# Product for the row maxima moved into the third chunk, scans paced by step, chunks and projection moved into the first and last steps of an attention loop

## The chip, the cores and the metric

The kernel runs on one core of one Trainium2 chip, in fp32. The metric is the device time of one execution in microseconds (us); lower is better. The core's engines are called PE (TensorE, matrix products), DVE (VectorE), ACT (ScalarE), POOL (GpSimd) and SP (SyncE, which here only issues DMA transfers). Each works through its own queue of instructions in order and waits on semaphores for the others.

## The reference, cut to what matters

The inputs are `x` [4, 256, 256] (4 batches, 256 tokens, width 256) and a context [4, 4096, 256]. In short:

```
x = x + cross_attention(x, ctx)     # 8 heads of 64, keys and values from 256 own rows and 4096 context rows
x = x + mixed(x)                    # per batch: a router picks 64 tokens for self-attention (16 heads);
                                    # the other 192 go through a state space model (512 channels, 16 states)
x = x + mixture_of_experts(x)       # 8 experts, 2 per token, hidden width 512
```

with layer norms ahead of the parts. In the state space model a recurrence h_t = dA_t * h_(t-1) + dBu_t runs along the 192 tokens for each channel and state. Cross-attention is by far the largest part, and the change lies in the loop that computes it.

## The kernel before: a loop over 128 steps

**Steps and groups.** The attention loop (L1546 to L1650) runs `n` from 0 to `N + 1`, `N` = 128. A group `G = n // 8` is one batch and one pair of heads (16 groups); a step `s = n % 8` is 32 query rows of it, for two heads. The 4352 keys lie as four quarters of 1088 on the partitions, so a score tile is 128 x 1088 for each head.

In step `n` the queues get, in this order:

- `scores(n)` (L1377): 32 + 4 products on PE into PSUM, tile `su`.
- `exps(n - 1)` (L1425): exponentials of the step before on ACT, with the negated maxima `nb` as bias.
- `copy_max(n)` (L1397): two passes of DVE over 128 x 1088 that copy `su` to `sp` and take the row maxima, then a small product into `mq` (L1410).
- pieces of other work on PE: key chunks of the next group (`k_chunk`, L1323) in s = 0, 6 and 7, value chunks of this group (`v_chunk`, L1354) in s = 2, 3 and 4, and in s = 1 and 5 `values` (L1442), the product of the exponentials with the values for four steps, cut into four pieces.
- `stat(n)` (L1412): the product of `mq` with `same`, which brings the four quarters' maxima together in a corner of `su`, and a reduction on DVE to `nb` (L1420). Since scores and this product share `su`, the scores of step n + 1 wait for `nb`.
- `turn(n - 1, 0)` and `turn(n - 1, 1)` (L1436): DVE transposes of the exponentials, which `values` reads.

Every chunk of keys or values reads 512 context rows, loaded over SP's queue into one of four buffers (`load_ctx`, L1235).

**Row sums and normalization.** When a group is through, `sums` and `spread` write the reciprocal row sums to DRAM, `fetch` (L1486, issued from ACT's queue in s = 1 of the next group) reads them back broadcast as `rs`, and `normalize` (L1502) multiplies the outputs `ao` by them on DVE. When a batch is through, `finish_batch` projects its four head pairs and adds to `x_sb`.

**Background work.** The mixed layer of batch b runs beside the attention of batch b + 1 (batch 3's in the expert stage behind the loop). It is written as Python generators: `slot(budget)` (L1169) at a few places of a step lets those go on whose due time (`yield delay, cost`) has come on a hand-kept clock `now` and whose cost on DVE fits the budget. `ssm_scan` (L702) is one of them: 32 scans per batch on DVE (`scan`, L743), each beside two exponentials for `da` on ACT (L731) and four passes on POOL (L736, L749, L751). A scan asks for 1.4 of a slot's budget; a second one in a slot is taken if 1.15 is left. `ssm_back` (L858) projects the result and adds it back; its first products are copied by ACT to `dsort` (L876).

The weights of a group come by `load_qk` (`wk2`), `load_self` (`wself`, one buffer, read by `k_self`, L1336) and `load_v`, all on SP's queue.

**After the loop** the expert stage begins (L1659); its weights reuse the memory of the loop's pools.

Of the kernel before, what the change touches and what calls it, by code (L numbers as in the profile page):

```python
# [14 lines left out]
P = 128  # L15
# [31 lines left out]
def perceiver_layer(ctx: ExitStack, tc: tile.TileContext, a: dict, out: bass.AP):  # L47
# [654 lines left out]
    def ssm_scan(b, st):  # L702

        SG = 2
        xc, delta, y = st["xc"], st["delta"], st["y"]
        das, dbs, bbs, cbs = {}, {}, {}, {}

        def load(k, o):

            if k < K:  # L710
                t = bg.tile(
                    [P, SG, NBOT], F32, tag=("bb", "cb")[o], name=("bb", "cb")[o], bufs=2
                )
                nc.sync.dma_start(
                    out=t, in_=st["bcd"][o, SG * k : SG * (k + 1), :].partition_broadcast(P)
                )
                (bbs, cbs)[o][k] = t

        def make(i):

            k, h = divmod(i, 2)
            if k == K:
                return
            tags = ((("r0", "r1"), ("r2", "r3")), (("wa", "wa"), ("ua", "r4")))[h]
            for j in range(2):
# [12 lines left out]
        def scan(k, m):  # L738

            da, db = das[k, m], dbs[k, m]  # L740
            nc.vector.memset(da[:, 1:, 0:1], 0.0)  # L741
# [12 lines left out]
        load(0, 0)  # L754
        load(0, 1)
        load(1, 0)
        while "attended" not in st:
            yield 1.0, 0
        make(0)
        make(1)  # L760
        yield 5.0, 1.4
        for i in range(2 * K):
            k, h = divmod(i, 2)
            for m in (2 * h, 2 * h + 1):
                if i or m:
                    if room[0] >= 1.15:
                        room[0] -= 1.15
                    else:
                        yield 2.2, 1.4
                scan(k, m)  # L770
                output(k, m)
            if h:
                load(k + 1, 1)
                load(k + 2, 0)
            make(i + 2)
# [82 lines left out]
    def ssm_back(b, st):  # L858
# [11 lines left out]
        for q, n in ((0, P), (1, NBOT - P)):  # L870
            for m in range(NDT):
                nc.tensor.matmul(
                    ps[:n, q * D : (q + 1) * D], zs[:, m, q * P : q * P + n],
                    ow[m // 2][:, m % 2, :], start=(m == 0), stop=(m == NDT - 1),
                )
            nc.scalar.copy(dsort[:n, q, :], ps[:n, q * D : (q + 1) * D])  # L876
        yield 2.5, 0.7

# [8 lines left out]
        nc.vector.tensor_tensor(xb, xb, ps, ALU.add)  # L887

    done = set()
    finished = set()  # L890
    late = {}

    def routed(b):
# [15 lines left out]
        ]  # L909
        if not late:  # L910
            yield 3.0, 0
        yield from st["late"] if late else ssm_scan(b, st)
        while "attended" not in st:
            yield 1.0, 0
        yield from ssm_back(b, st)
# [290 lines left out]
    with ExitStack() as s1:  # L1206
# [113 lines left out]
                ps.rearrange("p (k q i) -> p q k i", q=4, i=32),  # L1320
            )

        def k_chunk(G, g):  # L1323
# [5 lines left out]
            for c in range(KD):  # L1329
                nc.tensor.matmul(  # L1330
                    ps, wqk[G][:, 0, c, :], ct[:, c, :],
                    start=(c == 0), stop=(c == KD - 1),
                )
            keys_out(G, g * (CK // 4), ps)

        def k_self(G):  # L1336
# [14 lines left out]
                    ps[r, :T].rearrange("p (k q i) -> p q k i", q=4, i=32),  # L1351
                )

        def v_chunk(G, g):  # L1354

            b = G // NHP
            n = 4 if g < NCH else 2
            v = wk.tile([P, n, P], F32, tag=f"v{n}", name="v", bufs=NCH if g < NCH else 1)
            ps = ps_m.tile([P, 512], F32, tag="m", name="psv")
            if g < NCH:  # L1360
                ct = load_ctx(b, g)
            for i in range(n):
                for c in range(KD):
                    if g < NCH:
                        lhsT, w = ct[:, c, i * P : (i + 1) * P], 0
# [135 lines left out]
            ao = aos[divmod(G, NHP)][:, q]  # L1501
            nc.vector.tensor_tensor(ao, ao, rss[G][:, q], ALU.mult)  # L1502

        def project(b, half, ps, hps):
            for hp in hps:
                nc.tensor.matmul(
                    ps[:, half * D : (half + 1) * D],
                    aos[b, hp][:, half * P : (half + 1) * P], wo[:, hp, :],
                    start=(hp == 0), stop=(hp == NHP - 1),
                )  # L1510

        def add(b, half, ps):
            xb = x_sb[:, 2 * b + half, :]
            nc.vector.tensor_tensor(xb, xb, ps[:, half * D : (half + 1) * D], ALU.add)

        def finish_batch(b):

            yield 1.0, 0.9
            if b in psx:
                ps, done_hp = psx[b], NHP - 1  # L1520
            else:
                ps, done_hp = bank("psx"), 0
                project(b, 0, ps, range(NHP))
                add(b, 0, ps)
            project(b, 1, ps, range(done_hp, NHP))
            add(b, 1, ps)
            finished.add(b)

        psx = {}

        with tc.manual_schedule():
            norms = {}
# [13 lines left out]
            for n in range(N + 2):  # L1546
# [7 lines left out]
                if s % 4 == 1:  # L1554
                    m, took = n // 4 - 1, 1.95
                    if m >= 0:
                        pieces = [
                            lambda i=i: values(m, i, min(i + 9, NJ)) for i in range(0, NJ, 9)
                        ]
                elif 2 <= s <= 4 and G < NG:  # L1560
                    pieces = [
                        lambda g=g: v_chunk(G, g) for g in range(3 * s - 6, 3 * s - 3)
                    ]
                elif G + 1 < NG:
                    if s == 0:
                        wqk[G + 1] = load_qk(G + 1)
                        wself[G + 1] = load_self(G + 1)
                    pieces = {
                        0: [lambda g=g: k_chunk(G + 1, g) for g in range(3)],
                        6: [lambda g=g: k_chunk(G + 1, g) for g in range(3, 6)],  # L1570
                        7: [lambda: k_self(G + 1)]
                        + [lambda g=g: k_chunk(G + 1, g) for g in range(6, 8)],
                    }[s]


                tail = n >= N - 2

                def piece(i):
                    if i < len(pieces):
                        pieces[i]()  # L1580
                    if i < len(pieces) or tail:
                        now[0] += took

                if new:
                    scores(n)
# [2 lines left out]
                    exps(n - 1)  # L1588
                if new:
                    copy_max(n)  # L1590
                piece(0)
                if s % 4 != 1:
                    slot(1.3)
                    piece(1)
                    if old:
                        turn(n - 1, 0)
                    if new:
                        stat(n)
                        now[0] += 0.3
# [5 lines left out]
                    slot(1.3 if tail else 0.5)  # L1605
                    piece(2)
                    if s == 0 and n:
                        spread(G - 1)
                    slot(2.9)
                else:  # L1610
                    last = s == 1 and G
# [1 line left out]
                    if last:  # L1613
                        fetch(G - 1)
                    piece(1)
                    if new:
                        stat(n)
                        now[0] += 0.3
                    slot(2.8)
                    if last:  # L1620
                        normalize(m - 1)
                    if n == N + 1:

                        psx[B - 1] = bank("psx")
                        project(B - 1, 0, psx[B - 1], range(NHP))
                        add(B - 1, 0, psx[B - 1])
                        project(B - 1, 1, psx[B - 1], range(NHP - 1))
                    piece(2)
                    slot(1.5)
                    piece(3)  # L1630
                    if n > 4:
                        values_out(m)
                    if old:
                        turn(n - 1, 0)
                        turn(n - 1, 1)
# [344 lines left out]
```

## Time and profile before

| | |
|---|---|
| median of 3 runs | 1524.51 us (1523.6 to 1528.17) |
| the profiled execution's own time | 1526.89 us |
| its span | 1525.1 us |
| mean granted clock of PE | 0.981 |
| steps 0 to 127 of the loop | from 24.9 us to about 1242 us |
| expert stage | from about 1272 us on |
| DVE maxima pass, 128 x 1088 (L1403) | 256 of 1282 ns |
| DVE transpose, 128 x 1088 (L1440) | 256 of 1293 ns |
| DVE scan, 128 x 384 (L743) | 96 of 1317 ns |

The 96 scans are those of batches 0 to 2. "PE su L1415 <- DVE mq" reads: PE's product of line 1415, which writes `su`, waited for DVE's instruction that wrote `mq`. In a timeline the bracket holds the engine's idle time ahead of the line and what ended it; "issue" is time in which the engine waited for nothing that the profile shows.

### The profile page before, as it was taken

Reading aid. Unit: us, or ns where it says so; the run is one execution under the profiler, and the core shown is the slowest. Engines: PE = TensorE matmul, PEld = TensorE weight load, DVE = VectorE, ACT = ScalarE, POOL = GpSimd, SP = SyncE. Lnnn points to the kernel's source line nnn. Section 1 sums busy time; section 2 is a strip of 40 time slices with the busy share of each in tenths; the row PEclk is TensorE's granted clock in tenths of the full one; section 3 lists DMA queues with packets and bytes.
Section 4 is the critical chain, followed back from the end, with each engine's and each line's share of the span. In section 5 each row is a group of like instructions: output and inputs, shape, how many; then the busy total and the mean of one; then the engine's idle time right before and its main releaser. Section 6 shows DMA issues by size and latency. Waiting matters only on the chain.

```text
span 1525.1 us, 35283 instructions
## 1 busy us (share of the span) xinstructions
PE 1444.4 (95%) x14630; PEld 1021.4 (67%) x14630; DVE 1061.7 (70%) x1824; ACT 758.6 (50%) x1484; POOL 404.5 (27%) x467
## 2 busy tenths in 40 slices
PE   7999999999999999999999999999998968898999
PEld 3747566677666566676757575767575657888887
DVE  1656665656698986666889956666989663699353
ACT  3444454454665645455766544556655522553311
POOL 1000000000078860000598800001989101111020
PEclk9999999999999999999999999999999979999999
DMA  6555534424445343425454444352543333787661
GB/s 230 156 148 150 162 117 155 156 88 138 136 132 173 122 136 128 157 78 154 145 151 145 147 142 132 105 164 87 191 138 107 105 125 114 218 274 232 222 198 53
DMA packets 160352, 225.42 MB, mean 148 GB/s; under 512 B 15520, under 2 KB 78752, under 8 KB 160192
## 3 DMA queue, kind: packets, MB, share of 16 engines
q1 hardware_dynamic: 149632, 208.96, 43.5%
q10 hardware_dynamic: 9072, 10.13, 2.0%
q0 software_dynamic: 1488, 4.07, 0.9%
q8 instruction: 116, 1.90, 0.5%
q14 instruction: 44, 0.36, 0.1%
HBM read 218.66 MB, written 4.46 MB: 146 GB/s over the span
## 4 chain that ended last, share of the span: by engine, by line
PE 60%; DVE 20%; POOL 9%; issue 5%; DMA 3%; ACT 2%; SPq 0%; ACTq 0%; DVEq 0%; POOLq 0%
PE psv L1368 10%; PE su L1384 10%; PE po L1449 10%; PE psk L1330 9%; DVE sp L1403 6%; DVE db L743 4%; POOL y L751 3%; POOL db L749 3%; POOL db L736 3%; DVE pt L1440 3%; PE su L1391 2%; PE pde L1906 2%; PE pg L1893 2%; PE pu L1893 2%; DVE db L839 2%
## 5 line engine op out<-in xcount | busy, mean ns | idle before, releaser
L1403 DVE TENSOR_SCALAR_CACHE_REDUCE sp<-su 128x1088 f32<-128x1088 f32 x256 | 318.8, 1282 | 186.8 <-PE su L1391 186.8
L1440 DVE STREAM_TRANSPOSE pt<-sp 128x1088 f32<-128x1088 f32 x256 | 327.5, 1293 | 30.6 <-PE po L1449 26.6
L1431 ACT ACTIVATE sp<-sp,nb 128x1088 f32<-128x1088 f32 x256 | 305.1, 1195 | 15.7 <-DVE nb L1420 13.8
L1449 PE MATMUL po<-pt,v 128*64 128x128 f32 x4352 | 261.0, 278 | 2.1 <-DVE pt L1440 1.3
L1384 PE MATMUL su<-kt,qh 64*32 64x512 f32 x4096 | 256.3, 610 | 4.5 <-DVE nb L1420 4.0
L1330 PE MATMUL psk<-ctx,wk 128*128 128x512 f32 x512 | 245.9, 614 | 11.7 <-DMA ctx<-in_ctxT 8.0
L1368 PE MATMUL psv<-wv,ctx 128*128 128x128 f32 x2048 | 252.3, 280 | 0.0
L1449 PEld LDWEIGHTS po<-pt,v 128*64 128x64 f32 x4352 | 242.4, 139 | 11.9 <-issue 6.3
L1368 PEld LDWEIGHTS psv<-wv,ctx 128*128 128x128 f32 x2048 | 237.7, 193 | 11.1 <-issue 8.9
L1330 PEld LDWEIGHTS psk<-ctx,wk 128*128 128x128 f32 x512 | 91.7, 192 | 100.3 <-issue 92.6
L1318 ACT COPY kt<-psk 128x512 f32<-128x512 f32 x128 | 74.6, 585 | 155.8 <-PE psk L1330 155.5
L1384 PEld LDWEIGHTS su<-kt,qh 64*32 64x32 f32 x4096 | 63.1, 108 | 124.0 <-issue 95.5
L1372 ACT COPY v<-psv 128x512 f32<-128x512 f32 x144 | 79.4, 558 | 134.1 <-PE psv L1368 132.8
L751 POOL TENSOR_TENSOR y<-y,db 128x192 f32<-128x192 f32 x192 | 139.7, 728 | 15.0
L743 DVE TENSOR_TENSOR_SCAN db<-da,db 128x384 f32<-128x384 f32 x96 | 126.4, 1317 | 11.4 <-POOL y L751 0.5
L749 POOL TENSOR_TENSOR db<-db,cb 128x384 f32<-128x384 f32 x96 | 108.1, 1126 | 43.6 <-DVE da L741 43.6
L395 POOL TENSOR_TENSOR kbd<-qk,hmask 128x512 f32<-128x512 f32 x8 | 8.6, 1096 | 403.1 <-ACT qk L385 403.1
L731 ACT ACTIVATE da<-delta,A_log_sb 128x192 f32<-128x192 f32 x192 | 75.4, 447 | 51.0 <-DVE da L741 31.5
L736 POOL TENSOR_TENSOR db<-bb,xc 128x384 f32<-128x384 f32 x96 | 99.5, 1059 | 0.2
L1391 PEld LDWEIGHTS su<-kx,qh 128*32 128x32 f32 x1024 | 20.2, 108 | 109.4 <-issue 109.4
L1415 PEld LDWEIGHTS su<-mq,same 128*128 128x128 f32 x256 | 40.8, 190 | 66.3 <-DVE mq L1410 46.9
L1496 ACT COPY ao<-po 128x128 f32<-128x128 f32 x32 | 8.4, 264 | 139.5 <-PE po L1449 139.5
(297 smaller groups left out, 1569.3 us busy)
## 6 DMA issues: line engine op xcount, KB each, us to landing
ctx<-in_ctxT SPq DMA_DIRECT2D x256, 512.0 KB
gateT<-in_gateT SPq DMA_DIRECT2D x27, 512.0 KB
upT<-in_upT SPq DMA_DIRECT2D x27, 512.0 KB
downT<-in_downT SPq DMA_DIRECT2D x27, 512.0 KB
bb<-bcd SPq DMA_DIRECT2D x24, 192.0 KB
cb<-bcd SPq DMA_DIRECT2D x24, 192.0 KB
wv<-in_wv SPq DMA_DIRECT2D x32, 128.0 KB
in_w<-in_in_w SPq DMA_DIRECT2D x32, 128.0 KB
```

The lines of the kernel that those rows point to most:

```text
L736: nc.gpsimd.tensor_tensor(db, bbs[k], bc(xc[:, m, :], 1, SG), ALU.mult)
L743: nc.vector.tensor_tensor_scan(out=db, data0=da, data1=db, initial=0.0, op0=ALU.mult, op1=ALU.add,)
L749: nc.gpsimd.tensor_tensor(db, db, cbs[k], ALU.mult)
L751: nc.gpsimd.tensor_tensor(y[:, m, :], y[:, m, :], db[:, s, :], ALU.add)
L1330: nc.tensor.matmul(ps, wqk[G][:, 0, c, :], ct[:, c, :], start=(c == 0), stop=(c == KD - 1),)
L1368: nc.tensor.matmul(ps[:, i * P : (i + 1) * P], lhsT, wv[G][:, w, c, :], start=(c == 0), stop=(c == KD - 1),)
L1372: nc.scalar.copy(v.rearrange("p k d -> p (k d)"), ps[:, : n * P])
L1384: nc.tensor.matmul(su[q * 32 : (q + 1) * 32, SC[j] + lo : SC[j] + lo + 512], qT[r, s * 32 : (s + 1) * 32], kt[r, q, lo : lo + 512], start= ...
L1403: nc.vector.tensor_scalar(out=sps[n][j], in0=su[:, SU[j] : SU[j] + QK], scalar1=1.0, scalar2=None, op0=ALU.mult, op1=ALU.max, accum_out=nm ...
L1431: nc.scalar.activation(sps[n][j], sps[n][j], AF.Exp, bias=nbs[n][:, j : j + 1], accum_out=lss[b][:, hp, s, j : j + 1],)
L1440: nc.vector.transpose(pts[m, j][:, i, :], sps[n][j])
L1449: nc.tensor.matmul(pos[m][j * HD : (j + 1) * HD, :], vts[m // 2, k // 4][:, k % 4, j * HD : (j + 1) * HD], pts[m, j][:, :, kk * 32 : (kk + ...
```

## The change

1. **The maxima product.** `stat(n)` becomes `maxima()` and is called in the middle of the step's third chunk: after the first of two products of a `k_chunk`, or half way through a `v_chunk`. In s = 1 and 5 it comes after the third piece of `values`, and so in s = 1 after the `normalize` that used to follow it. In the last two steps it comes first.
2. **Pacing.** A slot of 1.3 opens ahead of the first piece, and what is left of it is offered again behind that. While a batch's scans run, the last slot of a step is 1.5 instead of 2.9 in s = 4 and 7 (from n = 97 on only in s = 4), and 1.5 instead of 2.8 in s = 1 and 5. The scan's delay is 1.9 instead of 2.2.
3. **First steps.** In group 0 the first two value chunks move to step 1, and `load_self` of the second group moves from s = 0 to s = 6.
4. **Last steps.** In the last group three value chunks move to its step 0 (n = 120). They lie in a key buffer that is free there (`vfirst`). The projection of the last batch's first three head pairs, and its add, move to n = 126.
5. **`ssm_back`.** The products of both halves come before the two copies to `dsort`.

```diff
-                        yield 2.2, 1.4
+                        yield 1.9, 1.4
...
+        for q, n in ((0, P), (1, NBOT - P)):
             nc.scalar.copy(dsort[:n, q, :], ps[:n, q * D : (q + 1) * D])
...
+        if not late:
+            scanning.add(b)
         yield from st["late"] if late else ssm_scan(b, st)
+        scanning.discard(b)
...
+                if mid and c == 0:
+                    mid()
...
+            if G == NG - 1 and g < 3:
+
+                if g == 0:
+                    vts["first"] = wke.tile([P, 4, SQ], F32, tag="kt", name="vfirst")
+                v = vts["first"][:, g, : n * P].rearrange("p (k d) -> p k d", d=P)
...
+                if mid and 2 * i == n - n % 4:
+                    mid()
...
+            add(b, project(b, range(NHP - 1 if b == B - 1 else 0, NHP)))
...
+                if G == 0 and s == 1:
+                    pieces = [lambda g=g: v_chunk(G, g) for g in range(2)]
+                elif s % 4 == 1:
...
+                elif G < NG and (2 <= s <= 4 or s == 0 and G == NG - 1):
+                    at = {0: (2, 5, 7, 9), NG - 1: (3, 6, 8, 9)}.get(G, (0, 3, 6, 9))
...
+                    if s == (6 if G == 0 else 0):
                         wself[G + 1] = load_self(G + 1)
...
+                if n == N - 2:
+
+                    part = project(B - 1, range(NHP - 1))
+                if tail:
+                    maxima()
+                slot(1.3)
                 piece(0)
                 if s % 4 != 1:
-                    slot(1.3)
+                    slot(room[0])
                     piece(1)
                     if old:
                         turn(n - 1, 0)
-                    if new:
-                        stat(n)
-                        now[0] += 0.3
+                    now[0] += 0.3
+                    slot(1.3 if tail else 0.5)
+                    if tail:
+                        piece(2)
+                    elif len(pieces) > 2:
+                        piece(2, mid=maxima)
+                    else:
+                        maxima()
...
+                    slot(1.5 if scanning and s in ((4,) if n > N - 32 else (4, 7)) else 2.9)
...
                     piece(1)
-                    if new:
-                        stat(n)
-                        now[0] += 0.3
-                    slot(2.8)
+                    now[0] += 0.3
+                    slot(1.5 if scanning else 2.8)
                     if last:
                         normalize(m - 1)
...
                     piece(2)
+                    if not tail:
+                        maxima()
                     slot(1.5)
```

More of the change, by code (lines that the diff above doesn't have):

```diff
@@ L889, in perceiver_layer @@
     done = set()
+    scanning = set()
     finished = set()
@@ L1321, in keys_out, with k_chunk @@
             )
-        def k_chunk(G, g):
+        def k_chunk(G, g, mid=None):
             b = G // NHP
@@ L1352, in k_self, with v_chunk @@
                 )
-        def v_chunk(G, g):
+        def v_chunk(G, g, mid=None):
             b = G // NHP
             n = 4 if g < NCH else 2
-            v = wk.tile([P, n, P], F32, tag=f"v{n}", name="v", bufs=NCH if g < NCH else 1)
+            if G == NG - 1 and g < 3:
[3 more added lines that the diff above has]
+            else:
+                v = wk.tile([P, n, P], F32, tag=f"v{n}", name="v", bufs=NCH if g < NCH else 1)
             ps = ps_m.tile([P, 512], F32, tag="m", name="psv")
@@ L1502, in normalize, with project, add @@
             nc.vector.tensor_tensor(ao, ao, rss[G][:, q], ALU.mult)
[L1504 to L1514, printed above, removed]
+        def project(b, hps):
+            ps = bank("psx")
+            for half in range(2):
+                for hp in hps:
+                    nc.tensor.matmul(
+                        ps[:, half * D : (half + 1) * D],
+                        aos[b, hp][:, half * P : (half + 1) * P], wo[:, hp, :],
+                        start=(hp == hps[0]), stop=(hp == hps[-1]),
+                    )
+            return ps
+        def add(b, ps):
+            for half in range(2):
+                xb = x_sb[:, 2 * b + half, :]
+                nc.vector.tensor_tensor(xb, xb, ps[:, half * D : (half + 1) * D], ALU.add)
         def finish_batch(b):
             yield 1.0, 0.9
[L1519 to L1526, printed above, removed]
+            add(b, project(b, range(NHP - 1 if b == B - 1 else 0, NHP)))
             finished.add(b)
-        psx = {}
         with tc.manual_schedule():
@@ L1553, in perceiver_layer @@
                     wv[G + 1] = load_v(G + 1)
-                if s % 4 == 1:
+                if G == 0 and s == 1:
+                    pieces = [lambda g=g: v_chunk(G, g) for g in range(2)]
+                elif s % 4 == 1:
                     m, took = n // 4 - 1, 1.95
[L1556 to L1560, printed above, removed]
-                    pieces = [
-                        lambda g=g: v_chunk(G, g) for g in range(3 * s - 6, 3 * s - 3)
+                    pieces = [
+                        lambda i=i: values(m, i, min(i + 9, NJ)) for i in range(0, NJ, 9)
+                    ]
+                elif G < NG and (2 <= s <= 4 or s == 0 and G == NG - 1):
+                    at = {0: (2, 5, 7, 9), NG - 1: (3, 6, 8, 9)}.get(G, (0, 3, 6, 9))
+                    if s == 0:
+                        at = (0, at[0])
+                    else:
+                        at = at[s - 2 : s]
+                    pieces = [
+                        lambda mid=None, g=g: v_chunk(G, g, mid) for g in range(*at)
                     ]
@@ L1566, in perceiver_layer, with piece, maxima @@
                         wqk[G + 1] = load_qk(G + 1)
+                    if s == (6 if G == 0 else 0):
                         wself[G + 1] = load_self(G + 1)
                     pieces = {
-                        0: [lambda g=g: k_chunk(G + 1, g) for g in range(3)],
-                        6: [lambda g=g: k_chunk(G + 1, g) for g in range(3, 6)],
+                        0: [lambda mid=None, g=g: k_chunk(G + 1, g, mid) for g in range(3)],
+                        6: [lambda mid=None, g=g: k_chunk(G + 1, g, mid) for g in range(3, 6)],
                         7: [lambda: k_self(G + 1)]
-                        + [lambda g=g: k_chunk(G + 1, g) for g in range(6, 8)],
+                        + [lambda mid=None, g=g: k_chunk(G + 1, g, mid) for g in range(6, 8)],
                     }[s]
                 tail = n >= N - 2
-                def piece(i):
+                def piece(i, **mid):
                     if i < len(pieces):
-                        pieces[i]()
+                        pieces[i](**mid)
                     if i < len(pieces) or tail:
                         now[0] += took
+                def maxima():
+                    if new:
+                        stat(n)
                 if new:
@@ L1596, in perceiver_layer @@
                         turn(n - 1, 0)
-                    if new:
-                        stat(n)
-                        now[0] += 0.3
+                    now[0] += 0.3
[4 more added lines that the diff above has]
+                        piece(2, mid=maxima)
+                    else:
+                        maxima()
                     if s == 0 and n:
@@ L1604, in perceiver_layer @@
                         turn(n - 1, 1)
-                    slot(1.3 if tail else 0.5)
-                    piece(2)
+                    if n == N - 2:
+                        add(B - 1, part)
                     if s == 0 and n:
                         spread(G - 1)
+                    slot(1.5 if scanning and s in ((4,) if n > N - 32 else (4, 7)) else 2.9)
+                elif n == 1:
+                    piece(1)
+                    now[0] += 0.3
+                    turn(0, 0)
+                    maxima()
+                    turn(0, 1)
                     slot(2.9)
@@ L1615, in perceiver_layer @@
                     piece(1)
-                    if new:
-                        stat(n)
-                        now[0] += 0.3
-                    slot(2.8)
+                    now[0] += 0.3
+                    slot(1.5 if scanning else 2.8)
                     if last:
                         normalize(m - 1)
[L1622 to L1627, printed above, removed]
                     piece(2)
+                    if not tail:
+                        maxima()
                     slot(1.5)
                     piece(3)
-                    if n > 4:
-                        values_out(m)
+                    values_out(m)
                     if old:
```

## The prediction

> **What bounds the kernel now.** I read the page first, then the waits of TensorE (PE) and VectorE (DVE), then PE's idle gaps over 0.3 us in order of time, then the timeline around the largest.
>
> ```profile
> PE 1444.4 (95%) x14630; PEld 1021.4 (67%) x14630; DVE 1061.7 (70%) x1824; ACT 758.6 (50%) x1484; POOL 404.5 (27%) x467
> ...
> DVE  1656665656698986666889956666989663699353
> ...
> PEclk9999999999999999999999999999999979999999
> ```
>
> PE is busy 95% of 1525.1 us, so all that reordering can win is its idle 81 us and time at a low clock. DVE's digits reach 9 where the scans of a batch run (slices 12 to 14, 20 to 22, 28 to 30), and there PE's gaps lie. PE's waits, then one of DVE's:
>
> ```profile
> PE su L1415 <- DVE mq L1410: 27.4, 19, 3.4
> PE psk L1330 <- DMA ctx<-in_ctxT: 8.0, 3, 6.3
> ...
> PE su L1415 <- DVE da L741: 4.5, 5, 2.1
> ...
> PE psk L1330 <- issue: 2.4, 1, 2.4
> ...
> PE pssd L872 <- ACT dsort L876: 1.8, 4, 0.5
> ```
> ```profile
> DVE ao L1502 <- DMA rs<-rd: 35.8, 13, 6.5
> ```
>
> The first and the third of PE's lines are one thing: the maxima product (L1415) reaches the head of PE before DVE has made `mq`, with a scan in front of it or behind it. In a quiet step there is no gap: the product comes at 5.8 to 6.3 us of the step, `mq` at 5.08. By batch the gaps are, from the trace: batch 0 0.38, 2.86, 2.10, 0.30, 1.13 (6.8 us); batch 1 2.84, 1.67, 1.14 (5.65); batch 2 2.86, 3.44, 0.72 (7.0): 19.5 us. The smaller ones of each batch's way back (0.9 + 0.9 + 0.6) and the end I take separately.
>
> A gap also costs clock. Stretches just after gaps of 2.38, 2.86 and 2.10 us (PE, PEld, DVE, ACT and POOL busy, then the granted clock):
>
> ```profile
> 30.40:33.70 3.30, 3.30 (x5) 1.35 (x4) 0.00 (x0) 0.59 (x1) 0.00 (x0) 0.50 0.75 286
> 482.40:485.80 3.40, 0.54 (x5) 0.49 (x5) 3.37 (x7) 0.59 (x1) 3.24 (x5) 1.00 0.80 201
> 511.70:515.00 3.30, 3.30 (x32) 3.28 (x33) 3.18 (x4) 2.37 (x6) 2.33 (x3) 0.50 0.29 77
> ```
>
> (the second holds its gap; no drop follows it). A drop lasts 3.4 us at 0.50, so it costs 1.7 us. The Trainium skill ("TensorE: Matmul & The Clock Gate", Part 1: The HAM clock gate) says to allow no idle gaps over about 3.4 us. By it the gaps here but one would be free of clock; the trace shows drops after 2.10 and 2.38 us, and I price a gap over 2 us at 1.7 more. By the rule the scan gaps are worth 19.5 us; by the trace, with five drops (511, 801, 829, 1119, 1170 us), 19.5 + 5 x 1.7 = 28 us.
>
> **The change, part by part.**
>
> *Start.* These lines show the order of SyncE's queue:
>
> ```profile
> 24.42 0.37 SPq L1217 DMA_DIRECT2D wself<-in_wk  x1
> ...
> 24.83 0.47 SPq L1217 DMA_DIRECT2D wself<-in_wq  x1
> ...
> 25.35 9.97 SPq L1235 DMA_DIRECT2D ctx<-in_ctxT  x6
> ...
> 29.55 5.37 PE L1330 MATMUL psk<-ctx,wk 128*128 128x512 f32 x8 [2.38 <-issue]
> ```
>
> The second group's `wself` has one buffer, waits for `k_self(0)`, and holds the ctx loads of step 0 behind it. Moved to step 6, where its two 128 KB loads wait for nothing and are due a step (some 8 us) later, it frees them: 2.38 + 1.7 = -4.1. If the ctx loads are late anyway, 0; the queue is otherwise empty, so I take -4.1.
>
> *Steps 1 to 4.* Step 1 has 3.1 us of gaps now. Two value chunks (8 us of PE) go there, but steps 3 and 4 keep 2 chunks each, and then scores, two maxima (1.28 each), product and `nb` set a floor of 6.5 to 7 us: 28.9 us for the four becomes 28.4, -0.5 (0 to -2.5). The chunks' 512 KB context loads go out a step earlier on SyncE's queue with them, past no other load, and into four buffers that PE frees by then; GpSimd's queue is passed by nothing. The last group's chunks into step 120 fill its 3.44 and 0.72, already counted.
>
> *Product in the third chunk.* It starts 0.4 to 0.8 us later in a step, so `mq` may be that much later. In quiet steps nothing is won. `nb` is later too, and scores(n+1), into the same banks, wait for it: it ends at about 7.2 of 7.8 us, still hidden. Turn(n-1,0) stands ahead of `nb` on DVE in both.
>
> *Pacing of the scans.* 32 scans per batch of 1.317 + 0.12 us each are spread over 16 steps (15 in batch 2) where they took 14. Eight steps then carry 16 x 1.44 = 23 us of scans and 8 x 5.45 us of maxima, `mq`, turns and `nb` = 43.6, in all 67.7 with sums and `ao`; PE needs 67.4 for eight steps. With 18 scans it was some 71. So DVE is level with PE, no longer behind it, and I take 24 of the 28 us away; the bounds are 14 (half the gaps stay, being burst by burst) and 28.
>
> *The new wait.* In steps 8G+1 the built order of DVE's queue is maxima, `mq`, scans, `ao`, `nb`, turns; it was maxima, `mq`, scan, `nb`, scans, `ao`. `ao` (L1502) waits for a DMA and `nb` is now queued behind it; scores(n+1), the whole of PE, wait for `nb`. In step 49 of before:
>
> ```profile
> 474.39 0.52 ACTq L1486 DMA_DIRECT2D rs<-rd  x1
> ...
> 478.79 0.99 DVE L1502 TENSOR_TENSOR ao<-ao,rs 128x128 f32<-128x128 f32 x1 [2.28 <-DMA rs<-rd]
> ```
>
> 4.4 us from issue to use, as in every such step. The issue sits on ACT's queue behind `da` activations, which wait for the first scan after `mq`: in both orders `mq` + 2.1. So `nb` ends at `mq` + 2.1 + 4.4 + 0.3 + 0.15 = `mq` + 7.0. With `mq` at 5.4 to 6.7 of the step that is 12.4 to 13.7, PE's work ends at 10.35: a gap of 2.0 to 3.4 us, with a drop of the clock 3.7 to 5.1. It comes in steps 49, 57, 81, 89, 113, 121, six times. In quiet steps the fetch is issued at 3.9, `ao` is at 8.3 to 8.5 and the product at 8.4 to 8.9 of 10.28 us: hidden. I take 4.2 x 6 = 25 us; bounds 12 and 31. In step 9 the same wait may cost 0.5. Net of pacing and wait: -24 + 25 = +1 (-16 to +17).
>
> *Way back of the scans.* Both products before the copies to `dsort` takes away the 0.46 us wait four times: -1.5, since the copies' next reader stands a step later. The normalization's chains move to other steps, at the same price.
>
> *End.* Three quarters of the last projection go into step 126, which has gaps of 3.03 and 3.03; there its 6 products (1.5 us) hide, and after the last values 2 products and 2 adds remain: -1.4 to the first expert. In step 126 itself -0.5: `pslg` with its normalization comes in its place. The first expert weights' buffers now come free with the last reader of "vfirst", some 21 us after the scores of step 127 begin instead of 4. They are due at 32; three loads of 512 KB at the 195 GB/s of the stage take 8: hidden by 3 us.
>
> Sum: -4.1 - 0.5 + 1 + 0.5 - 1.5 - 0.5 - 1.4 = -6.5 us. Against the profiled execution's 1526.89 (span 1525.1 and 1.8 around it) that is 1520.4; this execution lies 2.4 above the median of 1524.51, so on the median's scale 1518.
>
> **The rivals.**
>
> *`ao` comes in time.* If scans end sooner with less backlog, `mq` at 5.1 and the fetch ahead of the scan's `da` give a gap of a microsecond without a clock drop. Then -24 + 6 - 7.5 = -25: 1499; half of that, 1507, is likelier. For it: other steps have the fetch issued at 3.9. Against: in the built order of ACT's queue the fetch stands behind `da` in all six.
>
> *Slower.* The wait for `ao` also idles DVE: from the second scan's end (`mq` + 2.9) to `mq` + 6.5, 3.6 us, where before 2.28. Where DVE is level with PE this is not made up: the two scans queued after it push the next maxima, and gaps of 1 to 2 us follow in the step after. Then only 14 of 28 go away and the wait costs its upper 31: +17 - 7.5 = +9.5, 1534. It decides from 4.7 us per `ao` step on with half of the old gaps left. For it: step 50 of before has its 2.86 gap right after such a step.
>
> *No difference.* The six waits eat what the pacing gives, and the start's 4.1 is lost to later ctx waits (0.77 and 0.93 in step 8 are there now): 1522 to 1526.
>
> *Expert weights late.* If the three loads slip past 32 us, PE waits 3 to 5 us: 1522.
>
> **How the numbers follow.** This kernel's runs cannot tell less than 0.3% (4.6 us: 1519.9 to 1529.1) from no change. Forecast 1518, own range 1513 to 1524: 0.46. `ao` in time 0.15; slower 0.23; no difference 0.12; weights late 0.04. Of the forecast's own case two thirds (0.30) lie under 1519.9, the rest in the same band. So faster 0.30 + 0.15 = 0.45, same 0.16 + 0.12 + 0.04 = 0.32, slower 0.23. Range 1505 to 1532: it leaves out about half of the `ao`-in-time case below and half of the slower one above, 0.19.
>
> **What would show it.** The 2.38 gap at 27 us and the drop behind it gone; the wait of L1415 for `mq` from 27.4 + 4.5 to under 14; new waits of L1384 for `nb` of 2 to 3.4 us in steps 49, 57, 81, 89, 113, 121, with `nb` right behind `ao`; L872's wait gone; step 126 without two gaps of 3. I am wrong if the `nb` waits are missing (faster) or if waits for `mq` stay over 20 (slower).

## The result and the profile after

The changed kernel takes 1546.93 us (median of 4 runs, 1544.96 to 1551.05) against 1526.34 us for the kernel before (1523.6 to 1528.24) measured beside it: ratio 1.014, 95% interval 1.0111 to 1.0168. It is slower by some 20 us. The forecast was 1518 us with a range up to 1532, so neither the sign nor the range held. The profiled execution took 1546.88 us, its span is 1544.4 us, 19.3 us more than before.

The page's first rows, then the rows of DVE and of the clock by fortieths of the span:

```profile
PE 1443.6 (93%) x14630; PEld 1015.6 (66%) x14630; DVE 1058.6 (69%) x1826; ACT 756.6 (49%) x1484; POOL 390.8 (25%) x467
...
DVE  1656666675686976666869776756989873699453
...
PEclk9999999999998999999999999999999978999999
```

PE's busy time is what it was (1444.4 us before), so the 19 us are idle time: 101 us instead of 81. The pacing did spread the scans: those of batch 0 took 121.5 us before, in steps 45 to 57, and 153.3 us now, in steps 45 to 60. Part of the longer time is DVE's own waiting; with that taken away (experiment 2) it is 139.3 us. One of the two nines that DVE's row had in the stretches of batch 0 and of batch 1 is left in each. The waits of PE, and one of DVE's (waiting engine and line, engine and line waited for, us in total, times, longest):

```profile
PE su L1399 <- DVE da L741: 40.4, 6, 10.1
PE psk L1335 <- DMA ctx<-in_ctxT: 8.8, 3, 6.4
...
PE su L1430 <- DVE mq L1425: 5.6, 9, 2.8
...
PE psxb L1770 <- DMA xg<-x4d,tokens: 4.0, 1, 4.0
PE psk L1335 <- issue: 3.5, 3, 1.2
PE psk L1335 <- ACT kx L1356: 3.3, 3, 1.1
```
```profile
DVE ao L1517 <- DMA rs<-rd: 70.0, 15, 9.3
```

The maxima product's wait for `mq` shrank from 27.4 to 5.6 us, as the pacing was to bring, and L872's wait for `dsort` is no longer among the rows. In its place six waits of the *scores* (L1399) came, 40.4 us in all. They close steps 49, 57, 81, 89, 113 and 121, and measure 9.82, 6.14, 10.08, 6.14, 3.09 and 5.17 us. The row names the memset of `da` (L741), but that is merely the DVE instruction that ran just as PE went on; the timeline of step 49 shows what was waited for:

```profile
469.30 0.57 DVE L1425 TENSOR_TENSOR mq<-nm,quarter 128x8 f32<-128x8 f32 x1
...
469.88 0.32 SPq L714 DMA_DIRECT2D bb<-bcd  x1
...
470.29 2.20 SPq L1240 DMA_DIRECT2D ctx<-in_ctxT  x4
...
471.74 0.52 ACTq L1501 DMA_DIRECT2D rs<-rd  x1
...
481.89 0.29 DVE L1517 TENSOR_TENSOR ao<-ao,rs 128x128 f32<-128x128 f32 x1 [9.06 <-DMA rs<-rd]
482.10 0.16 DVE L1435 TENSOR_REDUCE nb<-su 128x2 f32<-128x8 f32 x1
```

`nb` starts as soon as `ao` is through, and `ao` waited 9.06 us for the broadcast row sums `rs`. These took 10.15 us from issue to use where the same transfer took 4.40 us in step 49 of before. Around the fetch SP issues four context loads of 512 KB, three of them 1.45 to 0.46 us ahead of it and the fourth 0.06 us behind it. In the kernel before, SP's queue reached its next context loads at 481.10 us, 6.7 us after the fetch of that step (474.39):

```profile
477.35 0.34 SPq L714 DMA_DIRECT2D cb<-bcd  x1
...
480.67 0.34 SPq L714 DMA_DIRECT2D bb<-bcd  x1
...
481.10 1.75 SPq L1235 DMA_DIRECT2D ctx<-in_ctxT  x3
```

Ahead of them in the queue stood a `cb` load and a `bb` load, which wait for POOL to be through with their buffers. With the scans spread, the `bb` load comes at 469.88, and the context loads behind it go out around the fetch.

The clock, by windows (PE, PEld, DVE, ACT, POOL busy, granted clock, DMA share, GB/s), at the old start stall, in the wait, in the middle of the wait, and after it:

```profile
30.40:33.70 3.30, 3.30 (x10) 1.36 (x8) 0.87 (x4) 1.08 (x2) 0.00 (x0) 1.00 0.59 171
471.70:481.80 10.10, 0.79 (x16) 0.54 (x10) 1.07 (x1) 1.56 (x4) 7.57 (x10) 0.75 0.74 232
473.70:478.70 5.00, 0.00 (x0) 0.00 (x0) 0.00 (x0) 0.01 (x1) 4.76 (x7) 0.80 1.01 370
482.20:485.60 3.40, 3.29 (x32) 0.68 (x32) 3.28 (x5) 2.17 (x6) 2.02 (x3) 0.50 0.02 5
```

At 30 us the clock is full now: the stall of step 0 is gone. In the long wait the DMA engines move 232 GB/s on average, and 5 GB/s after it. But for 5 us in its middle they are busy throughout (share 1.01), at 370 GB/s. By the packet records of the trace, `rs` moves nothing until 5.3 us after its issue, when 1.5 MB of SP's loads have gone through; in step 49 of before its first packet came 1.3 us after the issue. What `rs` waits for is the burst of loads: counted from the issue of the first of the four, it is in use after 11.4 to 11.8 us in steps 49, 57, 81, 89 and 113, although the fetch is issued anywhere from 1.4 to 5.3 us after that load.

By stages, in us against the kernel before (from the starts of the steps' scores; one profiled execution each). Steps 43 to 66 and 75 to 98 hold the scans of batches 0 and 1, 107 to 127 those of batch 2:

| steps | 0-1 | 1-5 | 5-9 | 9-43 | 43-66 | 66-75 | 75-98 | 98-107 | 107-127 | rest |
|---|---|---|---|---|---|---|---|---|---|---|
| changed | -4.1 | -1.6 | +2.1 | +0.6 | +10.6 | +2.3 | +7.5 | +2.3 | -3.2 | +1.7 |

The first column leaves the load phase out, which differed by +1.2.

### The profile page after: what moved, and what is told of

Same layout as the page of the kernel before. It is cut to its first block, busy times and chain, and to the rows that moved or that the text cites. A ratio compares the mean times of both kernels' runs of the same rounds, so it can differ in the third digit from the quotient of the medians.

```text
span 1544.4 us, 35257 instructions
## 1 busy us (share of the span) xinstructions
PE 1443.6 (93%) x14630; PEld 1015.6 (66%) x14630; DVE 1058.6 (69%) x1826; ACT 756.6 (49%) x1484; POOL 390.8 (25%) x467
## 4 chain that ended last, share of the span: by engine, by line
PE 72%; DVE 18%; DMA 5%; ACT 2%; issue 2%; POOL 1%; SPq 0%; ACTq 0%; DVEq 0%
PE su L1399 13%; PE psk L1335 13%; PE po L1464 13%; PE psv L1383 12%; DVE db L743 4%; DVE sp L1418 4%; DMA rs<-rd 3%; DVE pt L1455 3%; PE su L1406 2%; PE pde L1939 2%; PE pu L1926 2%; PE pg L1926 2%; DVE db L839 2%; PE psks L1348 2%; PE su L1430 1%
## 5 line engine op out<-in xcount | busy, mean ns | idle before, releaser
L1399 PE MATMUL su<-kt,qh 64*32 64x512 f32 x4096 | 261.2, 618 | 44.3 <-DVE da L741 40.4
L1464 PE MATMUL po<-pt,v 128*64 128x128 f32 x4256 | 250.8, 274 | 0.0
L1383 PEld LDWEIGHTS psv<-wv,ctx 128*128 128x128 f32 x2048 | 237.3, 193 | 10.6 <-issue 8.7
L1464 PEld LDWEIGHTS po<-pt,v 128*64 128x64 f32 x4256 | 233.4, 137 | 8.0 <-issue 6.0
L1399 PEld LDWEIGHTS su<-kt,qh 64*32 64x32 f32 x4096 | 63.3, 108 | 156.0 <-issue 77.9
L749 POOL TENSOR_TENSOR db<-db,cb 128x384 f32<-128x384 f32 x96 | 96.8, 1009 | 137.7 <-DVE da L741 98.7
L1435 DVE TENSOR_REDUCE nb<-su 128x2 f32<-128x8 f32 x128 | 20.1, 157 | 107.8 <-PE su L1430 107.6
```

What stands on the lines that cost most here:

```text
L1383: nc.tensor.matmul(ps[:, i * P : (i + 1) * P], lhsT, wv[G][:, w, c, :], start=(c == 0), stop=(c == KD - 1),)
L1399: nc.tensor.matmul(su[q * 32 : (q + 1) * 32, SC[j] + lo : SC[j] + lo + 512], qT[r, s * 32 : (s + 1) * 32], kt[r, q, lo : lo + 512], start= ...
L1464: nc.tensor.matmul(pos[m][j * HD : (j + 1) * HD, :], vts[m // 2, k // 4][:, k % 4, j * HD : (j + 1) * HD], pts[m, j][:, :, kk * 32 : (kk + ...
```

## The experiments

Theory A is the forecast's: the loss comes from `nb`'s place behind `ao`, with `rs` at its usual 4.4 us. Theory B, formed from the trace above: `rs` itself is slow, because context loads go out around it, and `ao`'s wait holds the whole of DVE's queue, whatever stands next in it.

Times are medians, ratios against the kernel before on the same chip with 95% intervals.

**1. `nb` ahead of `ao` again.**

```diff
-                    if last:
-                        normalize(m - 1)
                     piece(2)
                     if not tail:
                         maxima()
+                    if last:
+                        normalize(m - 1)
```

> The changed kernel, with the maxima product and nb put ahead of the normalization in the eight-step's second step again (only the order of these two on VectorE's queue differs). If it is nb that suffers by standing behind ao (theory A), PE's six waits for nb, 40 us, go away and the kernel comes to about 1505 us. If VectorE's whole queue is held by ao's wait for the transfer rs, which takes up to 10 us (theory B), whatever stands behind ao is late instead: the next step's maxima, and PE waits for mq in the steps after; at most 10 to 15 us are won: 1532 to 1537 us, with rs still landing 10 us after its issue in steps 49 and 81.

Measured: 1546.65 us, 1.0143 (1.0124 to 1.0162), the same as the changed kernel. The theory on which the forecast rested, that `nb` suffers by its place, falls in this form. In step 49 `nb` is now early, but DVE is held all the same:

```profile
470.34 0.13 DVE L1435 TENSOR_REDUCE nb<-su 128x2 f32<-128x8 f32 x1
...
479.57 0.29 DVE L1517 TENSOR_TENSOR ao<-ao,rs 128x128 f32<-128x128 f32 x1 [9.10 <-DMA rs<-rd]
...
482.04 1.94 PE L1383 MATMUL psv<-wv,ctx 128*128 128x128 f32 x8 [4.66 <-ACT ao L1511]
...
485.97 0.17 DVE L1425 TENSOR_TENSOR mq<-nm,quarter 128x8 f32<-128x8 f32 x1
486.19 0.60 PE L1430 MATMUL su<-mq,same 128*128 128x8 f32 x2 [2.21 <-DVE mq L1425]
```

PE goes through the scores of step 50 and then waits twice, 4.66 us for a copy on ACT and 2.21 us for the maxima. Whatever stands behind `ao` on DVE is late; which instruction it is matters little.

**2. The fetch at the start of the step.** `fetch(G - 1)` moves ahead of the first slot in s = 1, so ahead of the scans' activations on ACT's queue; `nb` stays behind `ao`.

```diff
+                if s == 1 and G:
+                    fetch(G - 1)
                 slot(1.3)
                 piece(0)
...
                     slot(1.5)
-                    if last:
-                        fetch(G - 1)
                     piece(1)
```

> The changed kernel, with the fetch of rs issued at the start of the step, ahead of the scans' activations on ScalarE's queue; nb stays behind ao. If the four context loads (2 MB) that SyncE issues just ahead of the fetch make rs late (theory B: the transfers share the DMA engines), the fetch now goes out some 2 us ahead of them and lands in about 4.4 us; the waits of 9.8 and 10.1 us in steps 49 and 81 fall under 1 and all six together from 40 to under 6 us: about 1508 to 1513 us. If the place of the fetch behind the activations is only 2 us of it (theory A as forecast), 6 x 2 = 12 us are won: about 1535 us.

Measured: 1515.34 us, 0.993 (0.991 to 0.9951): 31.6 us off the changed kernel by moving one transfer. Behind steps 49, 57, 81, 89 and 121 PE waits 1.0 us instead of 5 to 10; behind step 113 it still waits 2.90 us. In step 49:

```profile
465.04 0.52 ACTq L1501 DMA_DIRECT2D rs<-rd  x1
...
470.18 2.24 SPq L1240 DMA_DIRECT2D ctx<-in_ctxT  x4
...
472.64 0.61 DVE L1517 TENSOR_TENSOR ao<-ao,rs 128x128 f32<-128x128 f32 x1
```

There is no bracket behind `ao` any more: the fetch has gone out 5 us ahead of the loads, and `rs` lies there when DVE comes to it. The stages of the scans became -3.3, -6.1 and -6.0. In step 113 even the early fetch stands 2.1 to 3.6 us behind four context loads, and `rs` takes 7.75 us:

```profile
1091.61 2.26 SPq L1240 DMA_DIRECT2D ctx<-in_ctxT  x4
...
1095.20 0.51 ACTq L1501 DMA_DIRECT2D rs<-rd  x1
...
1102.95 0.29 DVE L1517 TENSOR_TENSOR ao<-ao,rs 128x128 f32<-128x128 f32 x1 [2.29 <-DMA rs<-rd]
```

This experiment takes away two things at once, the fetch's place behind the loads and its place behind the scans; experiments 6, 7 and 12 tell them apart.

**3. The kernel before with the normalization put first.** Only the order of `normalize(m - 1)` and `stat(n)` with its slot in s = 1 is changed.

```diff
+                    if last:
+                        normalize(m - 1)
                     if new:
                         stat(n)
                         now[0] += 0.3
                     slot(2.8)
-                    if last:
-                        normalize(m - 1)
```

> The kernel before, with nothing changed but the normalization put ahead of the maxima product and nb in the second step of each eight. If the order alone costs what the change showed (theory A), +30 to +40 us: 1555 to 1565 us. If the transfer is 4.4 us here, because the context loads go out after it (theory B), the waits for nb are 2 to 3.5 us in four of the scans' six steps (49, 81, 113, 121) and the rest is hidden: +8 to +16 us, 1533 to 1541 us, with no rs over 5 us from issue to use.

Measured: 1547.14 us, 1.014 (1.0117 to 1.0164). In the steps of the scans `rs` is at 4.4 to 4.7 us (in step 121 DVE came to it late), as theory B says, but the loss, 22.4 us, is more than its +8 to +16 and less than theory A's +30 to +40. The scores' waits are 3.18, 3.18 and 3.20 us in steps 49, 81 and 113; DVE itself stands 4.7 to 4.9 us there, with the scans behind it. And in steps 41, 73 and 105, which I had left out of the account, a product of the self-attention (L437) now waits 3.10, 3.53 and 2.77 us. So with `rs` at its usual time, the order of `ao` and `nb` alone is dear in this kernel.

**4. The start alone.** In the kernel before, `load_self` of the second group moves to step 6.

```diff
+                    if s == (6 if G == 0 else 0):
                         wself[G + 1] = load_self(G + 1)
```

> The kernel before, with nothing changed but the second group's wself loaded in step 6 instead of step 0. As forecast: the stall of 2.38 us in step 0 and the half clock behind it go, -4.1 us: 1520.5. The rival: the later context loads of step 8 take part of it back (the changed kernel waited 2.06 us there, the one before 1.7 in two places): -2 to -3, 1522.

Measured: 1520.02 us, 0.9973 (0.9958 to 0.9989), -4.7 us. Step 0 is 4.1 us shorter. The rival's loss in step 8 does not show: that step was 1.7 us shorter here, and between -1.9 and +2.2 us in the other profiles, so its loads scatter.

**5. The front slot only while scans run**, on top of experiment 2.

```diff
-                slot(1.3)
...
+                if scanning:
+                    slot(1.3)
                 piece(0)
                 if s % 4 != 1:
-                    slot(room[0])
+                    slot(room[0] if scanning else 1.3)
```

> The kernel with the early fetch (1515.3 us), and the slot of 1.3 ahead of the first piece opened only while scans run; else it stands behind the first piece as in the kernel before. If that slot, by putting the mixed layer's input products ahead of the self keys and key chunks, makes PE wait 1.10 and 1.18 us in the steps 39, 40, 71, 72, 103, 104 (theory), three times 2.27 us go away, and the last steps get the old order too: about 1508 us. If these waits come from the later maxima product, no change: 1515.

Measured: 1507.56 us, 0.9895 (0.9869 to 0.9921), 7.8 us off experiment 2. Steps 66 to 75 and 98 to 107 go from +2.3 to -1.5 each, and the waits of 1.10 and 1.18 us are gone. The end, though, is at +9.4: PE waits for the gathered tokens.

```profile
PE psxb L1771 <- DMA xg<-x4d,tokens: 9.0, 1, 9.0
```

**6. Three buffers for the context chunks**, on the changed kernel.

```diff
-        ctp = s1.enter_context(tc.tile_pool(name="xctx", bufs=4))
+        ctp = s1.enter_context(tc.tile_pool(name="xctx", bufs=3))
```

> The changed kernel with three buffers for the context chunks instead of four, so that at most three loads (1.5 MB) can stand ahead of the fetch. If the loads make rs late (theory B), rs comes some 2.5 us sooner in steps 49 and 81 (7.6 instead of 10.2 us from issue to use) and the six waits shrink from 40 to about 30 us: 1537 to 1542 us, if the chunks themselves come no later. If rs is slow for another reason, 10.2 us stay: 1547 or more.

Measured: 1540.71 us, 1.0108 (1.0078 to 1.0139). In step 49:

```profile
471.25 1.41 SPq L1240 DMA_DIRECT2D ctx<-in_ctxT  x3
...
472.75 0.52 ACTq L1501 DMA_DIRECT2D rs<-rd  x1
...
481.46 0.29 DVE L1517 TENSOR_TENSOR ao<-ao,rs 128x128 f32<-128x128 f32 x1 [7.67 <-DMA rs<-rd]
```

Three loads near the fetch instead of four make it 8.71 us instead of 10.15 in step 49, 8.98 instead of 10.40 in step 81, 6.71 instead of 7.95 in step 113, 5.03 instead of 6.12 in step 57 and 5.33 instead of 6.11 in step 89. From the first load's issue `rs` is now in use after 10.2 to 10.6 us. The direction is theory B's, in all of them; a load is worth 0.8 to 1.4 us, not 2.5. (As an estimate, 512 KB at the 370 GB/s of the wait's middle are 1.4 us.) The six waits of PE fell from 40.4 to 34.0 us, not to 30.

**7. The pacing alone**, in the kernel before: delay 1.9, the slots of 1.5 while scans run, the slot of 1.3 ahead of the first piece.

```diff
-                        yield 2.2, 1.4
+                        yield 1.9, 1.4
...
+                slot(1.3)
                 piece(0)
                 if s % 4 != 1:
-                    slot(1.3)
+                    slot(room[0])
...
-                    slot(2.9)
+                    slot(1.5 if scanning and s in ((4,) if n > N - 32 else (4, 7)) else 2.9)
...
-                    slot(2.8)
+                    slot(1.5 if scanning else 2.8)
```

> The kernel before with the pacing alone (delay 1.9, the slots of 1.5 while scans run, the slot of 1.3 ahead of the first piece); maxima product, first and last steps as before. As forecast (theory A), nb stands ahead of ao and the pacing alone wins its 24 us: 1500 us. If the pacing itself brings the context loads in front of the fetch and ao holds VectorE's queue (theory B), it alone loses what the change loses: +10 to +25 us, 1535 to 1550, with rs over 6 us from issue to use in steps 49, 57, 81 and 89.

Measured: 1562.18 us, 1.0249 (1.0224 to 1.0274). The pacing alone loses 37 us, more than the whole change, and it does so although `nb` stands ahead of `ao`:

```profile
472.54 10.46 SPq L1239 DMA_DIRECT2D ctx<-in_ctxT  x6
...
473.79 0.13 DVE L1424 TENSOR_REDUCE nb<-su 128x2 f32<-128x8 f32 x1
473.96 0.52 ACTq L1490 DMA_DIRECT2D rs<-rd  x1
...
484.43 0.29 DVE L1506 TENSOR_TENSOR ao<-ao,rs 128x128 f32<-128x128 f32 x1 [9.35 <-DMA rs<-rd]
...
491.05 0.59 PE L1419 MATMUL su<-mq,same 128*128 128x8 f32 x2 [8.46 <-DVE mq L1414]
```

The context loads go out from 1.4 us ahead of the fetch on, `rs` takes 10.46 us, and the loss shows as a wait of 8.46 us for the next step's maxima. In steps 81, 57 and 89 `rs` takes 10.43, 6.45 and 6.07 us. This is theory B. Not all of the 37 us is that, though: steps 66 to 75 and 98 to 107, which hold no scans, are 3.3 us longer each. And context loads are not the only ones that slow `rs`: in steps 41 and 105 none is issued within 7 us ahead of the fetch, but a `bb` load of 192 KB goes out less than 0.1 us ahead of it and a `cb` and a `bb` load within 0.9 us behind it, and `rs` takes 6.70 and 6.93 us. In steps 49 and 81, of this kernel and of the changed one, a `bb` load stands 1.9 us ahead of the fetch too; its share of the 10 us was not measured.

**8. The last steps alone**, in the kernel before: `vfirst`, the last group's chunks, the projection in step 126, the maxima product first in the last two steps; the lines are those of the change.

> The kernel before with the last steps' part alone (value chunks of the last group in its step 0, projection of three head pairs in step 126, the maxima product first in the last two steps). As forecast: the waits of 3.44 and 0.72 us in step 120 go, the end wins 1.4 us and step 126 some: -5 to -6 us, 1519 us. If the end loses as in the changed kernel (it gave 1.7 us back), only -3 to -4: 1521.

Measured: 1516.52 us, 0.9926 (0.99 to 0.9953), over 9 runs that spread from 1506.16 to 1519.01. In the profiled execution (1510.39 us) steps 107 to 127 are 8.4 us shorter and the rest 2.3 us. This part is better than expected, and by itself it doesn't lose at the end; but 2.5 us of the 8.4 also came in experiment 4, which touches nothing there.

**9. Pacing for two of the three batches**, on top of experiment 5.

```diff
-            scanning.add(b)
+            if b < B - 2:
+                scanning.add(b)
```

> The kernel with the early fetch and the late front slot (1507.6 us), with the pacing left out for the last of the three batches of scans, so that its way back and the sorting of tokens come two to three steps sooner again. If the end lost 9 us there because the paced scans push the sorting behind step 126 (theory), the end gives -2 instead of +9 and the stage before it stays at -8: about 1497 us. If the end's loss comes from the moved projection and the waits on vfirst, no change: 1507.

Measured: 1504.04 us, 0.987 (0.9851 to 0.9889), 3.5 us off experiment 5 and not the 10 expected. The end came back from +9.4 to +0.9 and the wait for the tokens is gone, but the stage before it went from -9.0 to -2.9: what the pacing wins in that stage it gives back at the end, where the sorting of the tokens comes later. Behind step 113 PE still waits 3.60 us, but for another reason than in experiment 2: no context load is near the fetch, and DVE, behind with its scans, does not wait for `rs`. This is the fastest kernel of the study.

**10. No pacing at all**, with the rest of experiment 5: the delay is 2.2 again, and `scanning` stays empty.

> The same kernel with no pacing at all (delay 2.2, the slots as in the kernel before); fetch early, maxima product late, first and last steps as changed. It shows what pacing is worth once the fetch is out of its way: by the forecast's 24 us for three batches, two of them 16 to 17, it is 1512 to 1514 us; if the late product already takes up most of VectorE's lag, 1500 us or less.

Measured: 1514.04 us, 0.993 (0.9907 to 0.9954). Against experiment 9 pacing two batches is worth 10.0 us, where the forecast's share for them was 16. The stages of batches 0 and 1 are +7.3 and -0.7 here and -3.0 and -4.2 there, so in its own stages pacing wins 13.8 us; the rest of the kernel behind step 127 is 5.7 us shorter here.

**11. The early fetch in the kernel before.** The move of experiment 2, with nothing else changed.

> The kernel before, with the fetch alone issued at the start of the step. VectorE waited 2.3 to 2.8 us for rs in steps 49, 81 and 113, and the gaps of 2.86, 2.84 and 2.86 us in the steps after follow from it: without the wait they shrink to about 0.5: 3 x 2.4 = -7, with two half-clock stretches -10: 1514 to 1518 us. If VectorE is behind there by its own work, no change: 1524.

Measured: 1517.95 us, 0.9961 (0.9946 to 0.9977), -6.3 us. DVE's waits for `rs` in steps 49, 81 and 113 fell from 2.3 to 2.8 us to 0.2 to 0.3; the stages of the scans gained 1.0, 4.0 and 1.8 us.

**12. The later product alone**, in the kernel before, behind the normalization in s = 1.

```diff
-                    if new:
-                        stat(n)
-                        now[0] += 0.3
+                    now[0] += 0.3
                     slot(2.8)
                     if last:
                         normalize(m - 1)
                     piece(2)
+                    if new:
+                        stat(n)
```

with the `mid` calls in the third chunk as in the change.

> The kernel before with the maxima product alone moved into the third chunk, and behind the normalization in the second step of each eight. Theory B: rs is not slowed here (no loads in front of the fetch), but ao holds nb and VectorE for 2 to 5 us in the steps of the scans, as with the normalization put first (1547 us), less 1 us a step of slack won elsewhere: 1530 to 1542 us. As forecast, the product's place wins nothing and the wait costs 12 to 25: 1537 to 1549.

Measured: 1543.62 us, 1.013 (1.011 to 1.0151), just above theory B's range and inside the forecast's. In step 49 `rs` takes 4.47 us and no context load is ahead of it, and yet:

```profile
475.98 0.52 ACTq L1490 DMA_DIRECT2D rs<-rd  x1
...
480.45 0.86 DVE L1506 TENSOR_TENSOR ao<-ao,rs 128x128 f32<-128x128 f32 x1 [2.35 <-DMA rs<-rd]
481.24 0.15 DVE L1424 TENSOR_REDUCE nb<-su 128x2 f32<-128x8 f32 x1
...
481.45 2.81 PE L1388 MATMUL su<-kt,qh 64*32 64x512 f32 x24 [5.24 <-DVE nb L1424]
```

PE waits 5.24 us because the fetch itself is late: it stands behind the scans' activations on ACT's queue, which follow `mq`, and `mq` comes 1.4 us later in the step than in before. So there are two ways to lose 20 us or more, a late issue (here) and a slow transfer (experiment 7). The change has both, and they do not add: experiments 4, 7, 8 and 12, which make up most of the change, come to +44 us together, the change to +20.6. That both losses end at the same `ao` is the likely reason.

## Why the prediction was wrong

**The step that failed** is the new wait's term: "4.4 us from issue to use, as in every such step", and with it "a gap of 2.0 to 3.4 us", six times. Place and count were right: six waits, in the six steps named, with `nb` behind `ao`. The size was not: 40.4 us of gaps where the working had 16 (6 x 2.7, before the clock's part). I had taken the transfer's time as a constant of the transfer. In before it was 4.4 to 5.1 us wherever DVE waited for it inside the loop, but there at most one context load stood within 4 us ahead of the fetch. In the changed kernel it is 10.15 and 10.40 us with four such loads from 1.4 us ahead of it to 0.9 us behind it, 7.95 with four 2 to 3.6 us ahead, 6.1 with four 3.7 to 5.2 us ahead. Experiments 2, 6 and 7 show the cause from three sides: moved ahead of the loads it holds nobody up; with one load fewer it is 0.8 to 1.4 us faster; and pacing alone, which shifts SP's queue, makes it slow. I had followed the moved loads on SP's own queue ("past no other load") and not asked what they do to a transfer from another queue.

In steps 49, 57, 81 and 89 the transfer's extra time is 15 of the 24 us by which the gaps are too long. The rest is a second term of the same sum: `mq` is through at 7.5 to 7.7 us of all six steps, where the working had 5.4 to 6.7, and the fetch goes out 2.4 us after the start of `mq` in four of them. In step 121 `rs` takes the 4.44 us of the working, and PE still waits 5.17 us. Why `mq` is later was not taken apart. Behind the six waits PE then ran 26 us at the half clock. As an estimate, that is another 13 us, so the six waits cost some 53 us where the sum had 25, and these 28 us are the forecast's whole miss of 27.

The Trainium skill ("DMA: Bandwidth & Descriptors", Issuing engines are not separate DMA queues) says that transfers issued by ACT, SP and POOL all run on the same 16 DMA engines and interleave. It would have raised the question, and this trace agrees with it: while `rs` waits, the 16 engines are at a share of 1.01 with SP's loads. The size, 0.8 to 1.4 us a load, is only in these runs.

**Why the range missed as well.** The upper end had six waits of 5.1 us, clock included; the longest were 10 us. The slower rival (1534) had the right mechanism in part, the idle DVE, but with the same 4.4 us in it. Experiments 3 and 12 show that even with 4.4 us the order `ao` before `nb` costs the kernel before 19 to 22 us, so the forecast was near for the wait that it had in mind.

**Pacing**, -24 us: the waits for `mq` that it was to shorten did go, and it wins, once the fetch is out of its way (10.0 us for two batches, experiment 10 against 9, where 16 were due). In the third batch it wins 6 us and costs 8.5 at the end (experiment 5 against 9). By itself, with the slot ahead of the first piece, it loses 37.

**The front slot** was not in the sum, except as "normalization's chains ... at the same price". It puts input products ahead of the keys in steps 39 to 40, 71 to 72 and 103 to 104, and cost 2.3 us each time; experiment 5 took it back.

**The end**, -1.4 - 0.5, measured +1.7. PE waits 5.84 us there for a transposition that stands behind the sorting on DVE, and 4.0 us for the gathered tokens. The projection is not to blame (experiment 8: -2.3); the later scans push the sorting into step 127. The expert weights were not late, so that rival did not come.

**Start** (-4.1): right, gap and clock, -4.1 in step 0 and -4.7 us in experiment 4. **Steps 1 to 4** (-0.5): -1.6; the same four steps differ by 1.6 us among kernels that don't touch them, so this says little. **Quiet steps** (0): right: a quiet s = 6 is 7.80 us and a quiet s = 3 is 8.01 us, before and after. **`dsort`** (-1.5): its four waits are gone; what that alone gave was not measured.

**The clock's price**, 1.7 us for a gap over 2 us: 2 us is no threshold. In before, the drop at 829 us, one of the five counted, follows a gap of 1.67 us.

What stays open: how much of the 10 us is the `bb` load's and how much the context loads'; why `mq` comes later in the scans' steps; and why the end of experiment 10 is 5.7 us shorter than that of experiment 9.

## What to carry to other kernels

Before moving work in time, look for the small transfers that an in-order engine waits for: their duration is set by what else is in flight, so ask which large loads the move will put ahead of them, on whatever queue. A wait at the head of an engine's queue holds all that follows; reordering what is behind it only changes the name of the loss (experiment 1), while issuing the transfer earlier takes it away (experiment 2), as long as the new place is not behind loads itself (step 113). Measure the parts one by one before judging the whole: here the one that was to win most lost most, and most of that loss went when one line was moved.

## What the runs showed of the hardware

- A 128 KB broadcast load took 4.4 to 5.1 us with at most one large load within 4 us ahead of it. It took over 10 us where four loads of 512 KB were issued from 1.4 us ahead of it to 0.9 us behind it (10.15 and 10.40 us in the changed kernel, 10.46 and 10.43 us with the pacing alone).
- With three of these loads it took 8.7 to 9.0 us.
- With four loads, it was in use 11.4 to 11.8 us after the issue of the first of them (changed kernel), with three 10.2 to 10.6 us (experiment 6), wherever within 5.3 us behind that first load it was issued itself.
- With no 512 KB load within 7 us ahead but three loads of 192 KB issued from 0.1 us ahead of it to 0.9 us behind it, it took 6.7 and 6.9 us (experiment 7, steps 41 and 105).
- In the waits of 9.8 and 10.1 us PE's granted clock fell to 0.50; it stayed there for 4.6 and 3.7 us after PE went on, and was 0.75 on average within the first of them.
